# Attention with the values' products of two steps one behind the other

## The chip, the cores and the metric

The kernel runs on one core of a Trainium2 chip. Its time is the device time of one execution in microseconds (us). The engines are TensorE (PE, with its weight loads PEld), VectorE (DVE), ScalarE (ACT), GpSimd (POOL) and SyncE (SP), which mostly issues DMA transfers. The profile is that of one execution.

## What is computed

Two layers run over 8 sequences of 512 tokens, 256 wide, in float32. Layer 0 is a state space block and a feed-forward layer with experts. Layer 1 is an attention with 16 heads of 16 and another layer with 7 experts. The change is in layer 1, whose attention is, for each sequence and head:

```python
qh, kh, vh = (heads(q), heads(k_rec), heads(v_rec))
scale = 1.0 / (jnp.sqrt(jnp.float32(D_MODEL)) + 1e-08)
scores = jnp.einsum('bhqd,bhkd->bhqk', qh, kh) * scale
...
decay = jnp.exp(-LAMBDA_DECAY * TIME_STEP * jnp.abs(idx[:, None] - idx[None, :]))
scores = scores * decay[None, None, :, :]
...
attn = jax.nn.softmax(scores, axis=-1)
out = jnp.einsum('bhqk,bhkd->bhqd', attn, vh)
...
return (out @ Wo, latent_kv)
```

The layer's result is x plus this attention's output plus the experts' output.

## The kernel before

Layer 0 comes first and takes up to about 1108 us. Then the attention of layer 1 runs as 128 steps, numbered n from 0 to 127: for each of 8 sequences (b), each of four groups of four heads (g), each of four chunks of 128 keys (c). So c is n modulo 4, and a group is done with a step whose number is odd. The order on every engine is written out by hand: within the manual schedule each engine runs its instructions in the order in which the loop issues them.

A step has these parts (class `Step`):

- `scores` (L1580, tile `s_ps`): four products, one for each head, of 128 keys by 512 queries. The four heads lie in four row groups of the array, 16 rows of each in use. Each product goes to one of four PSUM banks, which take turns (`bufs=4`). Then DVE reads each bank (L1583): it multiplies with the decay band, takes the largest value, and writes tile `s1` in SBUF (`s` in the profile). L1588 and L1590 make the bias `ng` and the weight `w`.
- `shares` (L1593) and `exps` (L1597) on ACT: the exponential of `w`, and of each of the four `s1` tiles in place.
- `weigh` (L1601) on DVE: the values' rows times `w`, into a tile `wv` out of a small set of shared ones.
- `values` (L1605, tile `o_ps`): four products of the weighted values (32 columns for each head, four column groups) with the exponentials. They add up in one PSUM bank over the four chunks of a group.

The loop is a pipeline of three: in iteration n it issues the scores of step n, the exponentials and `weigh` of step n - 1, and the values' products of step n - 2. Between the scores and the values' products it puts other work on PE, which this text calls the fill: the experts' products (`e_hp` L1423, `e_yp` L1436), transposes of their rows (`e_tp` L1400), and the output product of a finished sequence (`fin` L1540). Their results are copied by ACT (L1426, L1440, L1401, L1542), since PSUM has two more banks for all of these (`bank`, `bufs=2`). How much fill an iteration gets is set by `due()`, a share of the experts' work that grows evenly with n. The other two PSUM banks are those of `o_ps`. In the first few iterations the rest of the preparation (routing tables, L231, the last projections) takes the fill's place, and from n = 120 on there is little fill.

When a group is done, `divide` copies `o_ps` (L1698) and sends it through DRAM to divide it by the sums. The last sequence goes another way: `first_heads` and, after the loop, four objects `Ending`, one for each 128 tokens. Their parts are issued one after the other for all four: `out` (ACT copies a part of `o_ps` to `osq`, L1516), `divide` (transposes L1520 and L1521, then `columns`, whose last DVE instruction L1488 writes `oq`), `back` (transpose L1526 of `oq` and a copy), `project` (products L1532, sum, transfer out).

The part of the loop that the change touches:

```python
m = n - 2
if m >= 0:
    s = done[m]
    if s.c == 0:
        s_op = psum.tile([P, S], FP, name="o_ps", tag="o_ps", bufs=2)
    s.values(s_op)
```

Of the kernel before, what the change touches and what calls it, by code (L numbers as in the profile page):

```python
# [9 lines left out]
FP = mybir.dt.float32  # L10
# [7 lines left out]
P = 128  # L18
B, S, DM = 8, 512, 256
NT = B * S  # L20
NTILE = NT // P
TPB = S // P
# [23 lines left out]
AH, AD, DL = 16, 16, 64  # L46
# [12 lines left out]
def bc(ap, axis, shape):  # L59

    return ap.unsqueeze(axis).to_broadcast(shape)
# [3 lines left out]
def tile_kernel(ctx: ExitStack, tc: tile.TileContext, t, out: bass.AP):  # L65
# [48 lines left out]
    x1 = dram.tile([NT, DM], FP, name="x1", tag="x1")  # L114
# [453 lines left out]
    with ExitStack() as es:  # L568
        p1, p2, psum = m1, m2, mp
# [643 lines left out]
        N = len(chunk)  # L1213
# [157 lines left out]
    with tc.tile_pool(name="a1", bufs=1) as p1, tc.tile_pool(name="a2", bufs=2) as p2, tc.tile_pool(  # L1371
        name="ap", bufs=1, space=PSUM
# [108 lines left out]
        def columns(tq):  # L1481

            tq = tq.rearrange("p g (i r) -> p (g i) r", r=32)
            V.tensor_tensor(low[:, :8], low[:, :8], tq[:, :, AD], ALU.min)
            sm = p2.tile([P, 8], FP, name="smq", tag="smq")
            V.reciprocal(sm, tq[:, :, AD])
            oq = p2.tile([P, 8, AD], FP, name="oq", tag="oq")
            V.tensor_tensor(oq, tq[:, :, :AD], bc(sm, 2, [P, 8, AD]), ALU.mult)  # L1488
            return oq.rearrange("p h d -> p (h d)")

# [15 lines left out]
        class Ending:  # L1506
# [5 lines left out]
                self.at = slice(c * P, (c + 1) * P)  # L1512

            def out(self):
                self.last = p2.tile([P, P], FP, name="osq", tag="osq")
                A.copy(self.last, self.op[:, self.at])  # L1516

            def divide(self):
# [46 lines left out]
        class Step:  # L1565
# [7 lines left out]
            def scores(self):  # L1573

                cols = slice(self.c * P, (self.c + 1) * P)
                at = S - P - self.c * P
                sp = [psum.tile([P, S], FP, name="s_ps", tag="s_ps", bufs=4) for _ in range(4)]
                for i in range(4):
                    r = slice(32 * i, 32 * i + AD)
                    T.matmul(sp[i], self.k[r, cols], self.q[r, :], start=True, stop=True)  # L1580
                self.p = [p2.tile([P, S], FP, name="s1", tag="s1", bufs=12) for _ in range(4)]
                for i in range(4):
                    V.tensor_tensor_reduce(  # L1583
                        out=self.p[i], in0=sp[i], in1=band[:, at : at + S], scale=1.0,
                        scalar=KEEP, op0=ALU.mult, op1=ALU.max, accum_out=self.peak[:, i : i + 1],
                    )
                self.ng = p2.tile([P, 4], FP, name="ng", tag="ng", bufs=4)
                V.tensor_scalar(self.ng, self.peak, -1.0, KEEP, ALU.mult, ALU.add)  # L1588
                self.w = p2.tile([P, 4], FP, name="w", tag="w", bufs=4)
                V.tensor_scalar(self.w, self.peak, KEEP, MOST - KEEP, ALU.subtract, ALU.min)  # L1590
# [6 lines left out]
                    A.activation(self.p[i], self.p[i], AF.Exp, bias=self.ng[:, i : i + 1])  # L1597

            def weigh(self):
                self.wv = shared[done.index(self) % 3]  # L1600
                V.tensor_tensor(self.wv[:, :, :VH], self.v, bc(self.w, 2, [P, 4, VH]), ALU.mult)  # L1601

            def values(self, op):
# [12 lines left out]
        def exact():  # L1616

            nonlocal e1, e2
            G.memset(slots, 0.0)
            for _ in later[0]():  # L1620
                pass
            e1, e2 = given()
            for _ in experts():
                pass
            es.close()
            p3 = es.enter_context(tc.tile_pool(name="x", bufs=1, side="right"))
            for b in range(B):
                got = inputs_of(b)
                load_some(len(loads))
                xb = p3.tile([P, TPB, DM], FP, name="xb", tag="xb")  # L1630
                Y.dma_start(out=xb, in_=rows_of(xn1, b))
                xa = p3.tile([P, TPB, DM], FP, name="xa", tag="xa")
                Y.dma_start(out=xa, in_=rows_of(x1, b))
                for c in range(TPB):
                    V.scalar_tensor_tensor(
                        xb[:, c, :], xb[:, c, :], noop[:, b * TPB + c : b * TPB + c + 1], xa[:, c, :],
                        ALU.mult, ALU.add,
                    )
                oT = p1.tile([P, KC, S], FP, name="oT", tag="oT")
                for g in range(4):  # L1640
                    for c in range(TPB):
                        cols = slice(c * P, (c + 1) * P)
                        at = S - P - c * P
                        mx = p2.tile([P, 4], FP, name="mx", tag="w", bufs=4)
                        pT = []
                        for i in range(4):
                            r = slice(32 * i, 32 * i + AD)
                            sp = psum.tile([P, S], FP, name="x_ps", tag="s_ps", bufs=4)
                            T.matmul(sp, got["q"][g][r, cols], got["k"][g][r, :], start=True, stop=True)
                            p = p2.tile([P, S], FP, name="x1", tag="s1", bufs=12)  # L1650
                            V.tensor_scalar(p, sp, -CLAMP, CLAMP, ALU.max, ALU.min)
                            V.tensor_tensor_reduce(
                                out=p, in0=p, in1=band[:, at : at + S], scale=1.0,
                                scalar=-3.0e38, op0=ALU.mult, op1=ALU.max, accum_out=mx[:, i : i + 1],
                            )
                            V.tensor_scalar(mx[:, i : i + 1], mx[:, i : i + 1], -1.0, None, ALU.mult)
                            A.activation(p, p, AF.Exp, bias=mx[:, i : i + 1])
                            pp = bank("x_pp", [P, TPB, P])
                            for k in range(TPB):
                                T.transpose(pp[:, k, :], p[:, k * P : (k + 1) * P], ident)  # L1660
                            pT.append(p2.tile([P, TPB, P], FP, name="xT", tag="s1", bufs=12))
                            A.copy(pT[-1], pp)
                        op = psum.tile([P, 4, VH], FP, name="x_op", tag="o_ps", bufs=2)
                        for i in range(4):
                            h = 4 * g + i
                            for k in range(TPB):
                                T.matmul(
                                    op[:, i, :], pT[i][:, k, :], got["v"][:, k, h * VH : (h + 1) * VH],
                                    start=(k == 0), stop=(k == TPB - 1),
                                )  # L1670
                        sm = p2.tile([P, 4], FP, name="sm4", tag="w", bufs=4)
                        V.reciprocal(sm, op[:, :, AD])
                        o4 = p2.tile([P, 4, AD], FP, name="o4", tag="o4")
                        V.tensor_tensor(o4, op[:, :, :AD], bc(sm, 2, [P, 4, AD]), ALU.mult)
                        tp = bank("x_tp", [4 * AD, P])
                        T.transpose(tp, o4.rearrange("p h d -> p (h d)"), ident)
                        A.copy(oT[64 * (g % 2) : 64 * (g % 2) + 64, g // 2, cols], tp)
                for c in range(TPB):
                    fp = bank("x_fin", [P, DM])
                    for j in range(KC):  # L1680
                        T.matmul(fp, oT[:, j, c * P : (c + 1) * P], w_o[:, j, :], start=(j == 0), stop=(j == KC - 1))
                    V.tensor_tensor(xb[:, c, :], xb[:, c, :], fp, ALU.add)
                Y.dma_start(out=rows_of(out, b), in_=xb)
            es.close()

# [42 lines left out]
        with tc.manual_schedule(engines=ENGINES):  # L1728
# [7 lines left out]
            N = len(steps)  # L1736
            peaks = p1.tile([P, N * 4], FP, name="peaks", tag="peaks")
            low = p1.tile([P, 32], FP, name="low", tag="low")
            G.memset(low, 3.0e38)
            shared = [p1.tile([P, 4, 32], FP, name=f"wv{i}", tag=f"wv{i}") for i in range(3)]  # L1740
            for one in shared:
                G.memset(one, 0.0)
            vmax = p1.tile([P, B], FP, name="vmax", tag="vmax")
# [54 lines left out]
            done = []  # L1798
            tails = []
            for n in range(N + 2):  # L1800
# [28 lines left out]
                if last:  # L1829
# [6 lines left out]
                        last_rows(1)  # L1836
                    elif ready is not None and spent < due():
                        fill()
                m = n - 2
                if m >= 0:  # L1840
                    s = done[m]
                    if s.c == 0:
                        s_op = psum.tile([P, S], FP, name="o_ps", tag="o_ps", bufs=2)
                    s.values(s_op)
                    if s.c == TPB - 1:
                        if m == N - 1:
                            tails = [Ending(s.b, c, s_op, s.scratch[2]) for c in range(TPB)]
                        else:
                            chains.append(divide(s.b, s.g, s_op, *s.scratch))
                            next(chains[-1], None)  # L1850
# [116 lines left out]
```

## Time and profile before

| | us |
|---|---|
| median of 3 runs | 1734.75 (1732.07 to 1735.76) |
| profiled execution, its own time | 1730.83 |
| its span | 1729.1 |
| PE busy | 1567.4 (91%) |
| DVE busy | 1173.9 (68%) |
| ACT busy | 916.3 (53%) |
| 128x512 reduction of scores on DVE, L1583, x512 | 323.1 in all, 687 ns each |
| exponentials on ACT, L1597, x512 | 325.7 in all, 708 ns each |
| scores' products, L1580, x1024 | 166.7 in all, 678 ns each |
| values' products, L1605, x1024 | 145.4 in all, 640 ns each |

A line of the timeline gives the start, the time, the engine, the line of the kernel, the instruction, what it writes and reads, the tiles' sizes and how many follow each other; in brackets stands the idle time of the engine before it and what ended it. A product in float32 appears as two passes on PE, so a set of four is x8. Passes overlap: a set's time is read from start to start. In a row of the stretches the columns are the time, the busy time of PE, PEld, DVE, ACT and POOL with the number of instructions, the granted clock as a share of the full one, the DMA share and GB/s.

### The profile page before, as it was taken

The page shows a single profiled execution, that of the slowest core. Times are in us where ns is not written, and L with a number is a line of the kernel's source. Part 1 is how long each engine was busy: PE and PEld are TensorE (multiplying, and loading weights), DVE is VectorE, ACT ScalarE, POOL GpSimd, SP SyncE. Part 2 cuts the span into 40 slices and gives each one's busy share as a digit, 9 for nine tenths or more (in the row PEclk, how much of TensorE's full clock was granted, in tenths as well). Part 3 has the DMA queues.
Part 4 walks back from the last instruction along what each step waited for, and adds up shares of the span by engine and source line. Part 5 has one row for each costly group of instructions (what it writes and reads, how often), then busy time and mean ns, then how long its engine had stood idle before and what let it go on. Part 6 is the DMA issues. An engine that isn't in the chain of part 4 may idle for free.

```text
span 1729.1 us, 25738 instructions
## 1 busy us (share of the span) xinstructions
PE 1567.4 (91%) x8700; PEld 962.1 (56%) x8700; DVE 1173.9 (68%) x3067; ACT 916.3 (53%) x2173; POOL 571.0 (33%) x518
## 2 busy tenths in 40 slices
PE   6556799989999999999789898799999999999996
PEld 5323467767677677777445554564455445454442
DVE  6567675575576655875776925657777777777774
ACT  4232345345354453453544643327777777777773
POOL 0041456465465474654532422000211121112030
PEclk9777899999999999999989998759999999999986
DMA  8010445454564564564355624323433343344254
GB/s 295 21 55 0 152 159 198 161 187 180 166 212 146 175 196 148 181 221 137 83 115 163 179 87 145 105 74 114 135 86 111 97 133 97 90 119 141 57 98 125
DMA packets 131821, 231.09 MB, mean 134 GB/s; under 512 B 20109, under 2 KB 93839, under 8 KB 120528
## 3 DMA queue, kind: packets, MB, share of 16 engines
q1 hardware_dynamic: 101952, 119.46, 22.0%
q0 software_dynamic: 28656, 108.69, 20.6%
q8 instruction: 73, 1.20, 0.3%
q10 hardware_dynamic: 1072, 1.18, 0.3%
q14 instruction: 68, 0.56, 0.1%
HBM read 176.75 MB, written 53.58 MB: 133 GB/s over the span
## 4 chain that ended last, share of the span: by engine, by line
PE 71%; DVE 19%; ACT 4%; DMA 3%; issue 2%; POOL 0%; SPq 0%; ACTq 0%; DVEq 0%; POOLq 0%
PE s_ps L1580 7%; PE pj L946 7%; PE h_ps L640 7%; PE o_ps L1605 7%; PE y_ps L664 7%; PE e_hp L1423 5%; PE e_yp L1436 5%; DVE cv L959 3%; PE yd L1172 3%; PE op L1091 3%; PE seg L1134 3%; DVE s L1583 3%; PE sp L1202 2%; PE yoff L1190 2%; ACT s L1597 2%
## 5 line engine op out<-in xcount | busy, mean ns | idle before, releaser
L1583 DVE CUSTOM_DVE_ANT_0 s<-s_ps,band 128x512 f32<-128x512 f32 x512 | 323.1, 687 | 148.2 <-PE s_ps L1580 148.2
L1597 ACT ACTIVATE s<-s,ng 128x512 f32<-128x512 f32 x512 | 325.7, 708 | 0.0
L946 PE MATMUL pj<-xT,w_w_in 128*128 128x512 f32 x384 | 197.3, 640 | 9.5 <-DVE cv L959 5.5
L1441 POOL DMA_INDIRECT x<-e_yo,number x28 | 45.0, 1608 | 422.4 <-ACT e_yo L1440 342.2
L1580 PE MATMUL s_ps<-qT,kT 16*128 16x512 f32 x1024 | 166.7, 678 | 4.6 <-DMA kT<-kd 4.6
L959 DVE SCALAR_TENSOR_TENSOR cv<-pj,w_conv_w,cv 128x511 f32<-128x511 f32 (+2 forms) x192 | 143.2, 746 | 22.2 <-ACT cv L955 17.7
L1118 POOL TENSOR_TENSOR au<-da,half 128x512 f32<-128x512 f32 x64 | 76.6, 1197 | 228.7 <-PE seg L1134 156.7
L640 PEld LDWEIGHTS h_ps<-xdT,w 128*128 128x128 f32 x1152 | 138.8, 194 | 19.1 <-issue 18.3
L1605 PE MATMUL o_ps<-s,wv 128*32 128x512 f32 x1024 | 145.4, 640 | 1.2 <-ACT w L1593 1.2
L640 PE MATMUL h_ps<-xdT,w 128*128 128x128 f32 x1152 | 141.9, 277 | 0.5 <-DMA w<-in_w_dram,w_idx 0.5
L664 PE MATMUL y_ps<-w,hT 128*128 128x256 f32 x576 | 138.4, 384 | 0.0
L664 PEld LDWEIGHTS y_ps<-w,hT 128*128 128x128 f32 x576 | 108.3, 193 | 29.9 <-issue 16.1
L946 PEld LDWEIGHTS pj<-xT,w_w_in 128*128 128x128 f32 x384 | 69.8, 200 | 90.5 <-issue 80.1
L1580 PEld LDWEIGHTS s_ps<-qT,kT 16*128 16x128 f32 x1024 | 51.7, 193 | 119.0 <-DVE w L1590 51.1
L1423 PE MATMUL e_hp<-e_xdT,e_w 128*128 128x256 f32 x448 | 113.5, 391 | 3.7 <-ACT fo L1542 1.9
L1436 PE MATMUL e_yp<-e_w,e_hT 128*128 128x256 f32 x448 | 113.4, 392 | 1.5 <-ACT fo L1542 1.5
L1181 DVE TENSOR_TENSOR yT<-yT,yd 128x512 f32<-128x512 f32 (+1 forms) x64 | 43.8, 684 | 100.2 <-PE yd L1172 100.2
L1147 ACT ACTIVATE mt<-seg,mid 64x64 f32<-64x64 f32 x512 | 109.4, 309 | 0.8
L1436 PEld LDWEIGHTS e_yp<-e_w,e_hT 128*128 128x128 f32 x448 | 80.1, 189 | 50.6 <-issue 30.3
L1423 PEld LDWEIGHTS e_hp<-e_xdT,e_w 128*128 128x128 f32 x448 | 82.1, 191 | 40.8 <-ACT s L1597 15.2
L963 ACT ACTIVATE th<-cv 128x512 f32<-128x512 f32 x64 | 40.3, 630 | 116.7 <-DVE cv L959 108.0
L955 ACT ACTIVATE cv<-pj,w_conv_b,w_conv_w 128x512 f32<-128x512 f32 x64 | 49.8, 778 | 87.4 <-PE pj L946 83.4
(341 smaller groups left out, 2818.3 us busy)
## 6 DMA issues: line engine op xcount, KB each, us to landing
ex<-exd SPq DMA_DIRECT2D x96, 128.0 KB
fr<-fdd SPq DMA_DIRECT2D x64, 128.0 KB
e_w<-in_ei_dram SPq DMA_DIRECT2D x7, 1024.0 KB
od<-os SPq DMA_DIRECT2D x28, 256.0 KB
e_w<-in_eo_dram SPq DMA_DIRECT2D x7, 1024.0 KB
vd<-vt SPq DMA_DIRECT2D x16, 272.0 KB
vt<-vd SPq DMA_DIRECT2D x8, 544.0 KB
u<-in_u_dram SPq DMA_DIRECT2D x8, 512.0 KB
```

The source lines that it names most:

```text
L640: T.matmul(hp[:, i, :], w1[:, k * FF + f * P : k * FF + (f + 1) * P], xdT[:, k * P : (k + 1) * P], start=(k == 0), stop=(k == KC - 1),)
L664: T.matmul(yp, hT[f // 4][:, f % 4, :], w2[:, f * DM : (f + 1) * DM], start=(f == 0), stop=(f == FC - 1),)
L946: T.matmul(pj, w_in[:, k, o * P : (o + 1) * P], self.xT[:, k, :], start=(k == 0), stop=(k == KC - 1))
L959: V.scalar_tensor_tensor(cv[:, s:], pj[:, : S - s], conv_w[:, q, 3 - s : 4 - s], cv[:, s:], ALU.mult, ALU.add)
L1118: G.tensor_tensor(self.au, bc(da[:, d, self.i, :], 2, HH), bc(TRI[d], 1, HH), ALU.mult)
L1147: A.activation(mt[lo, over, h], seg[lo, over, h], AF.Exp, bias=mid[lo, self.i, h : h + 1])
L1423: T.matmul(hp, w1[:, k, f * P : (f + 1) * P], xdT[:, k, :], start=(k == 0), stop=(k == KC - 1))
L1436: T.matmul(yp, hT[:, f, c * P : (c + 1) * P], w2[:, f, :], start=(f == 0), stop=(f == FC - 1))
L1580: T.matmul(sp[i], self.k[r, cols], self.q[r, :], start=True, stop=True)
L1583: V.tensor_tensor_reduce(out=self.p[i], in0=sp[i], in1=band[:, at : at + S], scale=1.0, scalar=KEEP, op0=ALU.mult, op1=ALU.max, accum_out= ...
L1597: A.activation(self.p[i], self.p[i], AF.Exp, bias=self.ng[:, i : i + 1])
L1605: T.matmul(op[32 * i : 32 * i + 32, :], self.wv[:, i, :], self.p[i], start=(self.c == 0), stop=(self.c == TPB - 1),)
```

## The change

In an iteration with an even n below 128, the loop no longer issues values' products. In one with an odd n it issues those of the steps n - 3 and n - 2, one behind the other. After the last scores (n = 128 and 129) it goes on with one step each, as before. The `s1` tiles go from 12 buffers to 16 and `wv` from three to four. `oq` and `osq`, used only for the last sequence, go from two buffers to one.

```diff
@@ columns
-            oq = p2.tile([P, 8, AD], FP, name="oq", tag="oq")
+            oq = p2.tile([P, 8, AD], FP, name="oq", tag="oq", bufs=1)
@@ Ending.out
-                self.last = p2.tile([P, P], FP, name="osq", tag="osq")
+                self.last = p2.tile([P, P], FP, name="osq", tag="osq", bufs=1)
@@ Step.scores
-                self.p = [p2.tile([P, S], FP, name="s1", tag="s1", bufs=12) for _ in range(4)]
+                self.p = [p2.tile([P, S], FP, name="s1", tag="s1", bufs=16) for _ in range(4)]
@@ Step.weigh
-                self.wv = shared[done.index(self) % 3]
+                self.wv = shared[done.index(self) % 4]
...
-            shared = [p1.tile([P, 4, 32], FP, name=f"wv{i}", tag=f"wv{i}") for i in range(3)]
+            shared = [p1.tile([P, 4, 32], FP, name=f"wv{i}", tag=f"wv{i}") for i in range(4)]
@@ the loop
-                m = n - 2
-                if m >= 0:
+                for m in ((n - 3, n - 2) if n % 2 else ()) if n < N else (n - 2,):
+                    if m < 0:
+                        continue
                     s = done[m]
                     if s.c == 0:
                         s_op = psum.tile([P, S], FP, name="o_ps", tag="o_ps", bufs=2)
```

More of the change, by code (lines that the diff above doesn't have):

```diff
@@ L1649, in exact @@
                             T.matmul(sp, got["q"][g][r, cols], got["k"][g][r, :], start=True, stop=True)
-                            p = p2.tile([P, S], FP, name="x1", tag="s1", bufs=12)
+                            p = p2.tile([P, S], FP, name="x1", tag="s1", bufs=16)
                             V.tensor_scalar(p, sp, -CLAMP, CLAMP, ALU.max, ALU.min)
@@ L1660, in exact @@
                                 T.transpose(pp[:, k, :], p[:, k * P : (k + 1) * P], ident)
-                            pT.append(p2.tile([P, TPB, P], FP, name="xT", tag="s1", bufs=12))
+                            pT.append(p2.tile([P, TPB, P], FP, name="xT", tag="s1", bufs=16))
                             A.copy(pT[-1], pp)
```

## The prediction, made before the changed kernel was run

> **What bounds the kernel now.** I read the page's busy times first, then the stretches, because the change touches only the attention (its first score product starts at 1110.6 us). The page and one row of the stretches:
>
> ```profile
> span 1729.1 us, 25738 instructions
> PE 1567.4 (91%) x8700; PEld 962.1 (56%) x8700; DVE 1173.9 (68%) x3067; ACT 916.3 (53%) x2173; POOL 571.0 (33%) x518
> ```
> ```profile
> 1184.00:1662.00 478.00, 474.38 (x2808) 236.47 (x2804) 353.73 (x1292) 366.66 (x756) 69.29 (x51) 1.00 0.35 102
> ```
>
> In the stretch of steps 8 to 117 PE is busy 474.4 of 478.0 us at full clock, DVE 353.7, ACT 366.7. So PE carries the time, and whatever keeps it from its next product adds to the end. A step is four score products (S), expert and output products (the fill), four value products (O). Each product is recorded as two passes, so a set is x8. The timeline of step 32, an ordinary one:
>
> ```profile
> 1286.16 1.14 PE L1580 MATMUL s_ps<-qT,kT 16*128 16x512 f32 x8
> 1287.23 1.99 PE L1423 MATMUL e_hp<-e_xdT,e_w 128*128 128x256 f32 x8
> 1289.15 1.07 PE L1605 MATMUL o_ps<-s,wv 128*32 128x512 f32 x8
> 1289.15 0.69 DVE L1583 CUSTOM_DVE_ANT_0 s<-s_ps,band 128x512 f32<-128x512 f32 x1
> 1290.15 0.71 PE L1580 MATMUL s_ps<-qT,kT 16*128 16x512 f32 x4
> ```
>
> Start to start: S 1.07 us, fill 1.92, O 1.00, together 3.99. The fourth reduction of DVE (L1583) ends at 1289.84, 3.68 us after the scores began. The scores have four PSUM buffers, so each score product of the next step waits for the reduction that empties its bank. Today O covers that wait: the next scores come at 3.99. Where the fill is shorter, the cover is too thin. Step 36 and 37:
>
> ```profile
> 1305.51 1.06 PE L1605 MATMUL o_ps<-s,wv 128*32 128x512 f32 x8
> ...
> 1305.98 0.69 DVE L1583 CUSTOM_DVE_ANT_0 s<-s_ps,band 128x512 f32<-128x512 f32 x1
> ...
> 1306.50 1.35 PE L1580 MATMUL s_ps<-qT,kT 16*128 16x512 f32 x8
> ```
>
> Step 36 began at 1302.98 and its O stands at 2.53. The next scores start at 3.52, before the last reduction is over (1306.67), and their set takes 1.35 instead of 1.14: 0.21 us of waiting.
>
> **The change, part by part.** The order written out for PE differs in one thing: an even step issues no O, the odd step after it issues two sets. Fill, DVE, ACT and the DMA queues keep their order; the groups of four steps still end in an odd step, so the copy of o_ps, its chain of transfers and the expert work come in the same step as before. The two sets need exponentials two steps older, hence 16 buffers and a fourth wv. With 16 a reduction writes over a tile whose O was issued at least a step earlier, so these add no wait: 0.
>
> *What it saves.* O then S is 1.00 us start to start, while the two passes inside a set of O are 0.453 apart. Two sets one behind the other should take 4 x 0.453 plus one change to the next kind, 1.92 instead of 1.99: 0.07 per pair of steps. Bounds: 0, if the second set starts like any other, and 0.18, both changes around an O (0.09 each).
>
> *What it costs.* In an even step nothing stands between the fill and the next scores. PE reaches them at L, the distance from the step's first score to the end of its fill, which is where its O starts today. The fourth of them may start 0.06 us after the fourth reduction, at 3.74. The trace has such a case already, steps 120 and 121, where there is no fill and the next scores meet reductions under way:
>
> ```profile
> 1671.24 2.80 PE L1580 MATMUL s_ps<-qT,kT 16*128 16x512 f32 x8
> ...
> 1672.17 0.69 DVE L1583 CUSTOM_DVE_ANT_0 s<-s_ps,band 128x512 f32<-128x512 f32 x1
> ...
> 1672.92 0.29 PEld L1580 LDWEIGHTS s_ps<-qT,kT 16*128 16x128 f32 x2 [0.32 <-DVE peaks L1583]
> ...
> 1673.97 1.07 PE L1605 MATMUL o_ps<-s,wv 128*32 128x512 f32 x8
> ```
>
> The set lasts 2.80 us, its fourth product is loaded 0.06 after the fourth reduction's end (1672.86), and PE goes on 1.05 later. So an ordinary even step (L 2.99) waits until 3.74 where PE could have gone on at 3.01: 0.73 lost. What queues behind it on PE is the whole fill of the odd step, and after that two O; nobody gives it back, since PE is the bound. DVE has its slack (about 2 us) in the odd step, where it isn't needed. The pair takes 2.99 + 0.73 + 1.07 + 1.92 + 1.92 = 8.63 instead of 7.98.
>
> In general an even step loses 3.73 - L where that is positive; the pair saves 0.07, and a wait that today's odd step shows (as in step 37) is inside the new one. I read L and that wait off the timeline for the 55 even steps from 8 to 116:
> - 29 with a fill of 8 products, L 2.99 to 3.00: new waits 21.3, old ones 1.6, saved 2.0: +17.6 us.
> - 11 with 4 transposes and 4 products, L 2.52 to 2.57: new 13.0, old 2.0, saved 0.8: +10.2.
> - 1 with L 3.43: +0.2.
> - 14 with 12 products or output rows in the fill, L 3.86 and more: no wait, 0.07 saved each: -1.0.
>
> Together +27.0 us. Bounds: fills with output rows hold some 8 us of waits for ACT's copies today, which may shrink or grow when the odd scores come a step's O earlier: 19 to 33.
>
> *The ends.* Steps 0 to 7 have a clock of 0.5 in most of the stretch and fills over 4.8 us in their even steps: -0.3. Steps 118 and 119 are like the others, +0.3. From 120 on PE has little fill and DVE's reductions set the pace in either order, with O now behind the scores: the pair 120/121 reaches its end 0.9 later, the last pair's scores come earlier by about an O of that stage (1.86); I take +1 for all, between -3 and +4.
>
> *The single buffers of the last heads.* osq and oq go from two to one. The timeline of today's ending:
>
> ```profile
> 1714.49 0.30 PE L1526 MATMUL tb<-ident,oq 128*128 128x128 f32 x1
> ...
> 1715.15 0.29 DVE L1488 TENSOR_TENSOR oq<-tq,smq 128x128 f32<-128x128 f32 x1
> ...
> 1715.50 0.14 PEld L1526 LDWEIGHTS tb<-ident,oq 128*128 128x128 f32 x1 [0.21 <-DVE oq L1488]
> ```
>
> With two, the third oq waits for the first tb (1714.49 to 1715.15) and is turned 0.35 later: a round of 1.0 us. With one, each of four takes that round, and each osq copy waits for the transpose before it (0.68 a round, seen from 1713.38 to 1714.06). The last transpose of osq comes at 1715.42 instead of 1714.34, the first tb at 1715.6, the fourth three rounds on at 1718.6 instead of 1716.17: +2.4 us, all on the path, since the last projection stands behind it. Bounds 0 and 3.5.
>
> The sum is 27.0 - 0.3 + 0.3 + 1 + 2.4 = +30.4. The profiled execution took 1730.83 us (span 1729.1 and 1.7 around it), so it would take 1761. The median of the runs is 3.9 above that execution; I put the sum on it: 1765.
>
> [...] The granted clock fell to 0.50 at 1675.1, though in the 3.4 us before it PE was never without a product: those were the thin, spread scores of step 121. The 11 short pairs get such a spread, 2.3 us of it; had one in three the same effect and lasted 3.4 to 6.8 us at half clock as the falls of this trace do, 4 x 1.7 to 3.4 = 7 to 14 us come on top. I take none, because before 1675 no fall came in 490 us, with waits of up to 0.4 in the scores.
>
> [...]
>
> **The rivals.**
> - *The clock falls too* (0.12): the 7 to 14 us above, 1772 to 1780. For it: step 121. Against it: the spread is followed by 1.9 us of dense fill.
> - *The wait is mostly absorbed* (0.09): if half of the 27 us vanishes since today's waits for ACT in the odd steps go, and PE loses only 13 us, 1745 to 1752. Against it: PE idles 3.6 us in the whole stretch of 478 today, and no row shows more than about 8 us of waits hidden in its sets.
> - *Faster* (0.05): the scores don't wait, because DVE reaches them sooner; then 55 x 0.07 to 0.18 = 4 to 10 us are saved, 2.4 lost at the end, 1727 to 1733. It decides from a fourth reduction that ends by 2.95 instead of 3.68. Against it: the four reductions take 4 x 0.61 whatever the order, and cannot begin before the scores' first tile is ready, 1.16 after the start.
> - *No change* (0.02): the saving and the ending cancel, with no wait: within 0.2% (3.5 us), about what a measurement of this kernel can tell from none.
>
> **How the numbers follow.** The main case (0.72) runs from 1753 to 1774: the sum's 19 to 33 for the steps, the tail's -3 to +4 and the ending's 0 to 3.5 are not all at one end at once. Taking in half of each neighbouring rival gives 1750 to 1779. Slower by over 0.2% hold the main case, the clock and the absorbed wait: 0.93.
>
> **What would show it right or wrong.** After: score sets of odd steps that last about 1.9 us instead of 1.14, behind an even step's fill, with the weight load's idle time put down to L1583's peaks; pairs of ordinary steps 8.63 apart; value sets as x16 with 0.45 between the passes; PE's busy time hardly larger but its stretch longer, DVE's share lower. In the ending four rounds of oq and tb. Wrong if the odd scores run in 1.14 us: then the reductions are earlier than I read them, and the time falls. Wrong in size if the clock shows half anywhere between steps 8 and 118, or if fills with output rows change their waits for ACT.

## The result and the profile after

The changed kernel takes 1757.42 us, median of 6 runs (1755.67 to 1764.58). The kernel before, 6 runs on the same chip, takes 1730.01 (1724.62 to 1735.76). The ratio is 1.0148, with an interval of 1.0121 to 1.0176: the change costs 21 to 30 us. The forecast was 1765, between 1750 and 1779, and slower.

The profiled execution of after took 1764.58 us, 33.8 more than that of before. It is the slowest of its six, so the sum of the parts below is compared with this difference (33.7 between the two spans) and not with the medians. The head of its page:

```profile
span 1762.7 us, 25771 instructions
PE 1591.9 (90%) x8700; PEld 984.2 (56%) x8700; DVE 1174.7 (67%) x3067; ACT 915.5 (52%) x2173; POOL 574.3 (33%) x519
```

The rows of the stretches for steps 8 to 117, before and then after, each from the first score product of step 8 to that of step 118 (the row in the prediction, of 478.0 us, is some 4 us wider):

```profile
1184.50:1658.64 474.14, 470.52 (x2785) 234.56 (x2781) 350.37 (x1285) 363.01 (x748) 69.29 (x51) 1.00 0.35 103
```
```profile
1187.50:1689.00 501.50, 495.39 (x2788) 254.99 (x2784) 352.34 (x1287) 360.73 (x746) 70.23 (x51) 1.00 0.33 97
```

The stretch is 501.5 us long instead of 474.1. DVE and ACT are busy in it for about as long as before, and the clock is full. PE's busy time rises by 25 us, nearly all of the loss, although its products are the same: the wait inside its sets of four does not show as idle time, because the passes of the other three products fill it (the odd set below is recorded as 1.87 us of work, the even one as 1.14). The timeline of steps 32 and 33 shows this:

```profile
1295.65 1.14 PE L1580 MATMUL s_ps<-qT,kT 16*128 16x512 f32 x8
1296.72 1.99 PE L1423 MATMUL e_hp<-e_xdT,e_w 128*128 128x256 f32 x8
1298.65 1.87 PE L1580 MATMUL s_ps<-qT,kT 16*128 16x512 f32 x8
...
1298.65 0.69 DVE L1583 CUSTOM_DVE_ANT_0 s<-s_ps,band 128x512 f32<-128x512 f32 x1
...
1299.39 0.29 PEld L1580 LDWEIGHTS s_ps<-qT,kT 16*128 16x128 f32 x2 [0.32 <-DVE peaks L1583]
...
1300.45 1.99 PE L1423 MATMUL e_hp<-e_xdT,e_w 128*128 128x256 f32 x8
...
1302.37 1.92 PE L1605 MATMUL o_ps<-s,wv 128*32 128x512 f32 x16
...
1304.23 0.71 PE L1580 MATMUL s_ps<-qT,kT 16*128 16x512 f32 x4
```

Step 32 lasts 3.00 us to the next scores (1295.65 to 1298.65). Only then does DVE begin the fourth reduction, which ends at 1299.34. The fourth product's weights are loaded 0.05 us later, and the fill goes on 1.06 us after that, at 1300.45. So the odd set holds PE for 1.80 us instead of 1.07. Both value sets follow as one group of 16 passes. The pair takes 8.58 us; before it took 7.98.

### The profile page after: what moved, and what is told of

It is laid out like the page before. It is cut to its first block, busy times and chain, and to the rows that moved or that the text cites. A ratio compares the mean times of both kernels' runs of the same rounds, so it can differ in the third digit from the quotient of the medians.

```text
span 1762.7 us, 25771 instructions
## 1 busy us (share of the span) xinstructions
PE 1591.9 (90%) x8700; PEld 984.2 (56%) x8700; DVE 1174.7 (67%) x3067; ACT 915.5 (52%) x2173; POOL 574.3 (33%) x519
## 4 chain that ended last, share of the span: by engine, by line
PE 72%; DVE 17%; ACT 5%; issue 2%; DMA 2%; POOL 0%; SPq 0%; ACTq 0%; DVEq 0%; POOLq 0%
PE s_ps L1580 9%; PE pj L946 7%; PE o_ps L1605 7%; PE h_ps L640 7%; PE y_ps L664 7%; PE e_yp L1436 6%; PE e_hp L1423 5%; DVE cv L959 3%; PE seg L1134 3%; PE yd L1172 3%; PE op L1091 3%; ACT s L1597 3%; PE sp L1202 2%; PE yoff L1190 2%; DVE s L1583 2%
## 5 line engine op out<-in xcount | busy, mean ns | idle before, releaser
L1580 PE MATMUL s_ps<-qT,kT 16*128 16x512 f32 x1024 | 198.1, 674 | 6.1 <-DMA kT<-kd 4.5
L959 DVE SCALAR_TENSOR_TENSOR cv<-pj,w_conv_w,cv 128x511 f32<-128x511 f32 (+2 forms) x192 | 143.2, 746 | 20.5 <-ACT cv L955 16.0
L1605 PE MATMUL o_ps<-s,wv 128*32 128x512 f32 x1024 | 129.5, 626 | 0.0
L1580 PEld LDWEIGHTS s_ps<-qT,kT 16*128 16x128 f32 x1024 | 66.3, 191 | 101.1 <-issue 57.0
L1423 PE MATMUL e_hp<-e_xdT,e_w 128*128 128x256 f32 x448 | 117.2, 398 | 6.1 <-ACT fo L1542 3.4
```

Source lines behind the costliest of these rows:

```text
L959: V.scalar_tensor_tensor(cv[:, s:], pj[:, : S - s], conv_w[:, q, 3 - s : 4 - s], cv[:, s:], ALU.mult, ALU.add)
L1423: T.matmul(hp, w1[:, k, f * P : (f + 1) * P], xdT[:, k, :], start=(k == 0), stop=(k == KC - 1))
L1605: T.matmul(op[32 * i : 32 * i + 32, :], self.wv[:, i, :], self.p[i], start=(self.c == 0), stop=(self.c == TPB - 1),)
```

## Experiments

The stretch is that of steps 8 to 117 in the one profiled execution. The ordinary pair is steps 32/33; in the first two rows with the new order and three to one it is a pair whose 12 products don't wait for ACT, as 16/17. Ratios are to the kernel before, run on the same chip.

| kernel | ratio (interval) | stretch, us | ordinary pair, us |
|---|---|---|---|
| before | 1 | 474.1 | 7.98 |
| after | 1.0148 (1.0121 to 1.0176) | 501.5 | 8.58 |
| buffers alone | 1.0026 (1.0002 to 1.0050) | 474.8 | 7.98 |
| new order, two buffers | 1.0164 (1.0125 to 1.0203) | 501.4 | 8.58 |
| new order, five score banks | 1.0029 (1.0008 to 1.0050) | 481.6 | 7.96 |
| new order, three fill banks | 1.0093 (1.0063 to 1.0122) | 490.4 | 8.58 |
| old order, five score banks | 0.9999 (0.9980 to 1.0017) | 474.3 | 7.98 |
| old order, three fill banks | 0.9957 (0.9933 to 0.9980) | 468.3 | 7.98 |
| old order, fill three to one | 1.0159 (1.0129 to 1.0189) | 502.2 | 9.03 |
| new order, fill three to one | 0.9987 (0.9967 to 1.0007) | 477.9 | 7.85 |
| the same, five score banks | 0.9919 (0.9892 to 0.9946) | 475.1 | 7.85 |
| the same, three fill banks | 0.9868 (0.9837 to 0.9899) | 462.8 | 7.85 |

With the fill three to one, experts' work moves between the stretch and its neighbours. There the whole way from the first scores of step 0 to those of step 127 is compared: 593.1 us before, 621.1 after.

### Which part of the change: the buffers or the order

Buffers alone, with the loop of before:

```diff
-                for m in ((n - 3, n - 2) if n % 2 else ()) if n < N else (n - 2,):
-                    if m < 0:
-                        continue
+                m = n - 2
+                if m >= 0:
```

> The buffers of the change without its order: 16 tiles for exponentials, four wv, one oq and one osq, and the value products of step n - 2 in every iteration as before. If the loss comes from the order (the odd step's scores wait for the reductions of the even step), the pairs of ordinary steps stay at 7.98 us and only the ending grows, by the 1.8 us that it grew from the first transpose tq to the first output product (3.36 to 5.13 us): 1731 to 1734 with 1730 for the kernel before. If the larger set of tiles itself costs time (other places in SBUF, other waits), most of the 27 us of the stretch shows here: above 1745.

Measured: 1735.01 against 1731.62 us. The steps are as before. The ending, from the last value product to the first product `finq`, takes 5.54 us instead of 4.13. The stretch is 0.7 us longer. So 16 and four buffers cost next to nothing in the steps, and the single `oq` and `osq` cost 1.4 us in the ending. The interval of the runs (0.3 to 8.7 us) allows that and doesn't say it more finely.

The new order with two buffers each for `oq` and `osq`. The second `osq` takes its place out of the `s1` buffers:

```diff
-                self.last = p2.tile([P, P], FP, name="osq", tag="osq", bufs=1)
+                self.last = p2.tile([P, S], FP, name="osq", tag="s1", bufs=16)[:, :P]
-            oq = p2.tile([P, 8, AD], FP, name="oq", tag="oq", bufs=1)
+            oq = p2.tile([P, 8, AD], FP, name="oq", tag="oq")
```

> The changed kernel, with two oq again and with osq in tiles of the s1 set, which are free by then, so that neither waits in the ending. If the single buffers cost what the ending's rows say, 1.8 us go from the stretch between tq and the output products and about as much where the output products ran at half clock: 1753 to 1756 against 1757 for the changed kernel, and the steps stay as they are (pairs of 8.57 us). If the ending's growth is only the clock's, 1757.

Measured: 1759.52 us. The ending is back at 4.00, the stretch stays at 501.4. The order alone makes the loss. The run is some us above what was expected, and its interval overlaps that of after: the ending's 1.5 us can't be seen in the runs. All later versions of the new order have these two buffers.

### What the odd scores wait for

One more bank for the scores, taken from the values' sums:

```diff
-tag="s_ps", bufs=4
+tag="s_ps", bufs=5
-tag="o_ps", bufs=2
+tag="o_ps", bufs=1
```

> The order and buffers of e2, but five PSUM banks for scores and one for o_ps instead of four and two. The fourth score product of an odd step then waits for the third reduction of the even step (ends 3.07 us after that step's scores began) instead of the fourth (3.68). If the bank's release is what the odd scores wait for, ordinary pairs go from 8.57 to 7.96 us and the short ones lose their wait but for about 0.6 us: 29 x 0.61 + 11 x 0.61 = 24 us less than e2, 1729 to 1733. If the odd scores wait for something else of DVE or for the exponentials, it stays at 1753 or above; if one bank for o_ps brings a new wait for its copy by ACT, it shows in value products that wait in steps with c = 0.

The timeline of steps 32 and 33 of this version:

```profile
1285.14 1.99 PE L1423 MATMUL e_hp<-e_xdT,e_w 128*128 128x256 f32 x8
...
1287.07 1.26 PE L1580 MATMUL s_ps<-qT,kT 16*128 16x512 f32 x8
1287.07 0.69 DVE L1583 CUSTOM_DVE_ANT_0 s<-s_ps,band 128x512 f32<-128x512 f32 x1
...
1288.26 1.99 PE L1423 MATMUL e_hp<-e_xdT,e_w 128*128 128x256 f32 x8
...
1290.18 1.92 PE L1605 MATMUL o_ps<-s,wv 128*32 128x512 f32 x16
```

DVE's fourth reduction begins together with the odd scores, as in after, but now the fourth product waits for the third reduction. The set takes 1.19 us to the fill instead of 1.80, 0.61 less, which is one reduction's distance on DVE. The pair is 7.96, as expected. This shows that the wait is the one for the bank of the fourth product. The stretch falls by 20 us, not by the 24 expected: eight of the 29 ordinary pairs, those with 12 or more products in the odd step's fill, keep their length (pair 14/15: 9.95 in both). There the third group of products waits 0.85 us for a copy of ACT where it waited 0.25 in after. The runs give 1733.75 against 1731.62 us, where 1729 to 1733 was expected.

One more bank for the fill instead (scores four, values' sums one):

```diff
-tag="o_ps", bufs=2
+tag="o_ps", bufs=1
-name=name, tag="bank", bufs=2
+name=name, tag="bank", bufs=3
```

> The changed kernel (fill two and two, four banks for scores, osq out of the s1 set) with three banks for the fill and one for o_ps. The scores' wait is untouched: ordinary pairs stay at 8.57 us. In the odd steps with output rows the third product no longer waits for ACT's first copy: the value products come at 3.86 instead of 4.40 after the scores in steps 25, 41, 57, 73, 89 and 105, and up to 0.4 us earlier in steps 15, 23, 39, 55, 71, 81, 87 and 103: 4 to 7 us less in the stretch, 495 to 498 instead of 501.4, which would be the part of the loss that ACT's copies make and the sum left out. If these waits are not the banks', 501.

Step 25, which has output rows, in the timeline of after and then of this version:

```profile
1265.58 1.03 PE L1423 MATMUL e_hp<-e_xdT,e_w 128*128 128x256 f32 x4
1266.48 0.35 ACT L1542 COPY fo<-fin 128x256 f32<-128x256 f32 x1
...
1266.88 1.13 PE L1423 MATMUL e_hp<-e_xdT,e_w 128*128 128x256 f32 x4 [0.27 <-ACT fo L1542]
1267.94 1.93 PE L1605 MATMUL o_ps<-s,wv 128*32 128x512 f32 x16
```
```profile
1253.95 1.89 PE L1423 MATMUL e_hp<-e_xdT,e_w 128*128 128x256 f32 x8
1254.85 0.35 ACT L1542 COPY fo<-fin 128x256 f32<-128x256 f32 x1
1255.77 1.92 PE L1605 MATMUL o_ps<-s,wv 128*32 128x512 f32 x16
```

In after, the second group of `e_hp` needs the bank that `fin` had, and ACT copies that one late, behind the exponentials. The value products come 4.40 us after the step's scores (1263.54). With a third bank the two groups run as one, the value products come after 3.85 us (scores at 1251.92), and the copy is off the path. The ordinary pairs stay at 8.58, the stretch falls by 11 us, more than the 4 to 7 expected. So the new order holds at least 11 us of waits for ACT's copies. The runs give 1745.26 against 1728.37 us.

The same two edits in the old order separate what the new order added. Five score banks there:

> The kernel before, in its own order, with five PSUM banks for scores and one for o_ps. If the scores' only wait is for the bank, the few waits that the order before already has (0.16 to 0.43 us in 20 odd steps of the stretch of steps 8 to 117) go, 4 to 6 us: 474 becomes 468 to 470 us, and the run 1725 to 1729 against 1731.6. If the single o_ps makes the value products wait for ACT's copy of it, steps with c = 0 grow and the stretch is 474 or more.

Measured: no difference (1728.62 against 1728.37 us). The waits of the short pairs go (step 13: 3.99 instead of 4.20), but later waits for ACT's copies give them back (step 15: 6.13 instead of 5.72). The expected 4 to 6 us didn't come. Three fill banks in the old order:

> The order of before, with one bank for the values' sums and three for the fill. It asks whose the 11 us of waits for ACT's copies are that the three fill banks took out of the new order. If about 8 us of them are in the old order too (some 0.7 us in each of the steps 15, 23, 25 and their like), the stretch from step 8 to step 118 falls from 474 to 466 to 470 us and the runs to 1720 to 1725. If the waits belong to the new order alone, 1726 to 1732. If the single bank for the values' sums makes the first product of a new group wait for the copy of the one before it, it is slower than before, 1735 or more.

Measured: 1724.05 against 1732.75 us, and the stretch is 5.8 us shorter. In this execution the pair 110/111 is 1.46 us longer than before, since DVE stood idle for a late transfer ahead of step 110's reductions:

```profile
1620.65 0.69 DVE L1723 TENSOR_TENSOR oT<-oT,rb 128x512 f32<-128x512 f32 x1 [2.56 <-DMA rb<-rd]
```

Without that pair the stretch is 7.3 us shorter. So of the 11 us some 6 to 7 are in the old order, and 4 to 5 came with the new one.

### Is it the thin cover

If the wait comes from a cover that is too thin, more fill in the even step and less in the odd one takes it away, with nothing else changed. In the new order:

```diff
-                    fill(1), fill(1)
+                    for _ in range(1 if n % 2 else 3):
+                        fill(1 if n % 2 else 2)
```

> The order and buffers of e2, with the fill shared out differently: three calls in an even step, one in an odd one, instead of two and two. Nothing of DVE, of the banks or of the value products changes. If the wait is only a matter of how soon PE is back at the scores, an even step of 12 products (L 3.86) covers the reductions: ordinary pairs go from 8.57 to about 7.84 us, 0.14 below the 7.98 of the kernel before, and the time falls to 1720 to 1730. If two value sets behind each other are dear in themselves, or the odd step's exponentials come too late, it stays above 1745. ACT's copies of three products in one step may bring waits of 0.1 to 0.5 us each in the steps with output rows.

Steps 32 and 33 in its timeline:

```profile
1276.38 1.14 PE L1580 MATMUL s_ps<-qT,kT 16*128 16x512 f32 x8
1277.46 3.11 PE L1423 MATMUL e_hp<-e_xdT,e_w 128*128 128x256 f32 x12
1280.49 1.14 PE L1580 MATMUL s_ps<-qT,kT 16*128 16x512 f32 x8
1281.57 1.13 PE L1423 MATMUL e_hp<-e_xdT,e_w 128*128 128x256 f32 x4
1282.63 1.92 PE L1605 MATMUL o_ps<-s,wv 128*32 128x512 f32 x16
```

The odd scores come 4.11 us after the even ones, behind the fourth reduction, and their set lasts 1.14. In this pair ACT's copies stretch the 12 products (3.03 us); in pairs where they do not, the pair takes 3.86 + 3.99 = 7.85. From step 0 to step 127 it takes 584.7 us instead of 621.1: the loss of the change is gone, and in the runs (1726.92 against 1731.62 us) it can't be told from before.

The same fill in the old order, where the odd step now has only four products and its O ahead of the next even scores:

> The kernel before, in its own order (one set of value products in each step), with the fill shared three to one. No value products are paired here. If it is the cover between two sets of scores that counts, the odd steps are now the short ones: 1.07 + 1.06 + 1.00 = 3.13 us until the scores of the next even step, whose fourth product may start at 3.73, so an odd step with one unit of fill (some 29 of 55) waits 0.6 us: +17 us in the stretch, 1745 to 1752. If pairing the value products is what is dear, there is nothing of it here: 1729 to 1735.

```profile
1290.94 1.74 PE L1580 MATMUL s_ps<-qT,kT 16*128 16x512 f32 x8
1292.61 1.99 PE L1423 MATMUL e_hp<-e_xdT,e_w 128*128 128x256 f32 x8
1294.79 1.13 PE L1423 MATMUL e_hp<-e_xdT,e_w 128*128 128x256 f32 x4 [0.18 <-ACT e_hT L1426]
1295.85 1.07 PE L1605 MATMUL o_ps<-s,wv 128*32 128x512 f32 x8
1296.84 1.14 PE L1580 MATMUL s_ps<-qT,kT 16*128 16x512 f32 x8
1297.91 1.13 PE L1423 MATMUL e_hp<-e_xdT,e_w 128*128 128x256 f32 x4
```

Now the even set waits: 1.67 us to its fill instead of 1.07, the expected 0.60. With no two sets of values' products put together, the old order loses as much as the change did: 1756.49 against 1728.37. Of the 28 us in the stretch, 33 of the 55 even sets hold 19.8 by this wait, while the 3.6 us of waits in today's odd sets are gone. So it isn't the pairing that costs, but the time between one set of scores and the next. The size was missed (up to 1752 was expected): some 12 us more lie in the fill, where 12 products ahead of one copy also wait for ACT, here 3.24 us instead of 2.79.

### A version that beats both

Three to one, with the fifth bank for the scores:

> Value products in pairs, fill shared three to one, osq out of the s1 set, and five banks for scores: the candidate that should beat both kernels. Beside the kernel with three to one and four banks (477.9 us for steps 8 to 117, of which 0.36 us are still waited for in each of some 11 pairs with transposes), those 11 waits go: 4 us less, 1721 to 1725 against 1731.6 for the kernel before. If it is not faster than that kernel's 1726.9, the rest is waits for ACT's copies, which the banks for scores don't touch.

Measured: 1715.58 against 1728.37 us, below the 1721 to 1725 expected, though the stretch fell by 2.8 us and not by 4; where the rest of that gain lies stays open. No set of scores waits any more in the stretch; ACT's copies still cost (step 25: 6.25 us). Three to one, with the third bank for the fill:

> The new order with the fill three to one, two buffers for oq and osq, one bank for the values' sums and three for the fill; the scores keep four banks. Against the version with five banks for the scores it lacks the cover of the short pairs (a wait of 0.36 us in each of 11, about 4 us) and should be free of ACT's waits in the steps with output rows (10 us or less). If the two add up: 1709 to 1717, as fast as that version or a little faster. If with three to one the copies no longer stand in the way, the third bank brings nothing, and it is 1717 to 1727, slower than that version by the short pairs' waits.

Its row of the stretches:

```profile
1181.90:1644.70 462.80, 462.80 (x2792) 243.31 (x2788) 350.92 (x1286) 361.34 (x750) 69.03 (x51) 1.00 0.36 105
```

Measured: 1709.84 against 1732.75 us, 17 to 28 us faster than before. PE has no idle time in the stretch; waits inside sets of scores remain, 6.1 us in all: about 0.3 us in the odd set of each short pair and 0.2 to 0.6 in eight others. The time lies where it was expected if the two repairs add up. Not all of it comes from the pairing: the third fill bank alone gave 8.7 us in the old order. An ordinary pair takes 7.85 us, 0.13 less than in the old order: that is what the pairing is worth once its wait is covered.

## Why the prediction held, point by point

The parts of the sum against the two profiled executions:

| part | forecast, us | measured, us |
|---|---|---|
| before the attention | 0 | +1.7 |
| steps 0 to 7 | -0.3 | +1.3 |
| steps 8 to 117 | +27.0 | +27.3 |
| of these, 29 ordinary pairs | +17.6 | +16.6 |
| 11 short pairs | +10.2 | +9.4 |
| 1 with L 3.43 | +0.2 | +0.2 |
| 14 pairs with long fills | -1.0 | +1.1 |
| steps 118 and 119 | +0.3 | +0.3 |
| step 120 to the last value product | +1 | -0.4 |
| ending, to the first `finq` | +2.4 | +1.5 |
| the last projection | 0 | +1.7 |
| the rest, to the end | 0 | +0.3 |
| sum | +30.4 | +33.7 |

*The mechanism* was right in its place, its size and its condition. The fourth product of the odd set starts when the fourth reduction is over, as read off the steps 120 and 121 of before, and the loss is 3.73 - L. From their start to the next product, the odd sets of the stretch hold PE for 30.8 us more than before. The runs with five banks and with the two fills three to one show each side of that condition.

*Two terms were off and cancelled.* The saving was taken as 0.07 us per pair and is 0.14: the four rounds of passes of step 33 in after start 0.453, 0.429 and 0.429 apart, while the forecast took 0.453 for each step from round to round. That makes 55 x 0.07 = 3.8 us less. (Its own figures, 1.00 and 0.453, make 1.91 for two sets and a saving of 0.09; it wrote 1.92 and 0.07.) Against it, the 14 pairs with long fills did not win as a whole: in six of them (24/25, 40/41, 56/57, 72/73, 88/89, 104/105) the odd step's products meet ACT's copy of `fin` a step's O earlier, and the pair loses 0.2 to 0.4 us. The forecast named these waits as a bound and left them out of the sum; the three fill banks show them at 11 us against 6 to 7 before. The eight ordinary pairs with 12 or more products in the odd step lose 0.24 to 0.92 us, the other 21 lose 0.59 or 0.60. That the sum comes to 27.3 against 27.0 is partly luck.

*The ends* were guesses and are off by about 1 to 2 us each. In the ending, the timeline of after shows the rounds:

```profile
1745.90 0.29 DVE L1488 TENSOR_TENSOR oq<-tq,smq 128x128 f32<-128x128 f32 x1 [1.20 <-PE tb L1526]
1746.34 0.30 PE L1526 MATMUL tb<-ident,oq 128*128 128x128 f32 x1 [0.48 <-DVE oq L1488]
1746.68 0.29 DVE L1488 TENSOR_TENSOR oq<-tq,smq 128x128 f32<-128x128 f32 x1 [0.30 <-PE tb L1526]
...
1747.97 4.23 PE L1532 MATMUL finq<-w_w_o,oT 128*128 128x256 f32 x11
```

The next `oq` begins 0.04 us after the transpose's end, and a round takes 0.78 where the forecast had 1.0: the 0.66 us from the first `tb` to the third `oq` in before were not that wait alone. On the other hand the products `finq` ran at half clock (0.5 from 1748.18 for 3.4 us), and from the first of them to the end of the last it took 5.31 us instead of 3.62. Nothing in the sum had that. It was 3.62 in the new order with two buffers and in the run of the buffers alone, so it belongs to this execution or to the ending's gaps together with it; that stays open.

*The level.* The forecast of 1765 put 30.4 us on a median of 1734.75, three runs. Six runs have 1730.01, and the medians differ by 27.4. So 4.7 of the 7.6 us by which it was too high come from the level.

*The rivals.* The clock did not fall in the stretch (1.00 in the row above) although its sets of scores lasted 1.8 us and more in some 40 pairs; the longest wait in a set is 1.2 us. What sets off a fall is not shown. In before the clock is 0.50 from 1675.1 on, behind 3.40 us in all of which PE was busy:

```profile
1671.70:1675.10 3.40, 3.40 (x18) 1.17 (x18) 3.37 (x14) 1.86 (x4) 3.40 (x5) 1.00 1.23 195
1675.10:1678.50 3.40, 3.36 (x10) 1.34 (x10) 2.52 (x11) 3.40 (x8) 3.30 (x3) 0.50 1.23 186
```

The forecast priced this rival by falls of 3.4 to 6.8 us, such as the one from 381.5 to 384.9 in before (0.50); the two that follow the stretch in before lasted 13.7 and 20.5. The waits for ACT did not absorb the loss: they grew by 4 to 5 us. The scores did not become faster, as DVE does the same reductions (0.69 us each) at the same distance from the scores' start: in step 32 the fourth ends 3.69 us after it, 3.68 in before.

*The profile's signs* came as told but for one: PE's busy time was to grow hardly at all, and in the stretch it took 25 of the 27 us, since three of four products spread over the wait.

## What to carry to other kernels

Work between two uses of a buffer is a cover for whoever empties it, as the fill and O are here for DVE: before moving it, set the distance that is left (here 2.99 us) against the moment of release (3.73), step by step, since the mean of a busy engine and a slack one (PE 470.5 and DVE 350.4 of 474.1 us) shows nothing of it. When an order is good but uncovers a wait, other work can be put in the gap (here three units of fill to one: 1726.92 us instead of 1759.52), and the order's small gain then remains (0.13 us a pair). PE fills two kinds of banks here that others empty, and with five score banks in the old order the wait taken away at one came back at the other (step 13 is 0.21 us shorter, step 15 0.41 longer); the kind that then shows the wait is the one to try another bank on, as the third fill bank did here (1724.05 against 1732.75 us).

## What the runs showed of the hardware

Two sets of values' products one behind the other ran closer than one alone lets see: in step 33 of after the rounds of the first set are 0.453 us apart, those across and inside the second set 0.429, and the change to the scores takes 0.543 from the last round's start.

While the fourth score product waited, the other row groups went on: in step 33 of after, the second pass of the first product starts at 1299.179, before the first pass of the fourth at 1299.397. That is why the wait inside such a set looks like work in PE's busy time (495.4 us in the stretch, 470.5 before).
